# Output weights kept dequantised in DRAM, last loads on GpSimd's queue, first block projected in the last head

## The chip, the core and the metric

The kernel runs on one core of a Trainium2 chip. The metric is the device time of one execution in microseconds. The core has five engines with a queue of instructions each: TensorE (PE, with its weight loads as PEld), VectorE (DVE), ScalarE (ACT), GpSimd (POOL) and SyncE (SP). SP, ACT and POOL can issue DMA transfers; each has its own queue, and all transfers run on the same 16 DMA engines.

## What is computed

The input x has 2048 rows of 256. The block is a sandwich of attention and a mixture of experts:

```python
h  = layernorm(x)
q, k, v = h @ Wq + bq, h @ Wk + bk, h @ Wv + bv      # 16 heads of 128
o  = concat_h softmax(q_h k_h^T / sqrt(128)) v_h      # 2048 x 2048 scores per head
x  = x + layernorm(o @ Wo + bo)
g  = top-2 router of 8 experts on layernorm(x)
x  = x + layernorm(sum_e g_e * (silu(n @ Wg_e) * (n @ Wu_e)) @ Wd_e),  n = layernorm(x)
```

Wq, Wk, Wv and Wo come as codes (float32 values of a 4-bit grid) and a scale for each block of 32 rows; a weight is code times scale. Wo has 2048 rows (16 heads of 128) and 256 columns.

## The kernel before

**The loop.** The attention goes head by head, and in each head over 16 steps of 128 query rows (`for g in range(NS + 2)`, L740; h is the head, t the step). A step computes two halves of scores (`scores_half`, L478) on PE; DVE takes the maximum (L488), ACT the exponential (L499). In the next step ACT makes the float16 high part `ph` (L513) and DVE the low part `pl` in two halves (L528), the second one in the step after. SP transposes each with a DMA into `pth` (L516) and `ptl` (L534). `pl` has two buffers.

**PV.** Four steps make a block of 512 query rows. The product with V for a block is cut into eight units of six matmuls (`pv_part`, L546), two of them per step, and lags the scores by 13 units (`PVLAG`, L700). After the eighth unit POOL splits the result into two float16 parts `o` (L570, L571) and its queue stores them to `ot_d` in DRAM (L574). When the loop ends, the whole last block of head 15 (units `UEND + 1` to `UEND + 8`) is still to do.

**Side work.** `fill` (L582) puts the projections of q, k and v for this or the next head between the scores; `proj_qk` (L213) with `wide` leaves its cast and low part to POOL (L235, L236). `weight_steps` (L140) loads and dequantises Wq, Wk and Wv for the next pair of heads on POOL. Wo is loaded in eight pieces of two heads: pieces 0 to 2 in head 14 from POOL's queue (`load_wo_part`, L611), pieces 3 to 7 in head 15 (`late`, L709; `load_wo`, L628) with the scales from ACT's queue and the codes from SP's. POOL multiplies each piece into `wo` (L645). `late` also loads Wg and splits it (`split_gu`, L679), makes the bias row (`bias_row`, L647) and loads five of block 0's attention outputs back (`load_oi`, L689), all of it from SP's queue, on which the transposes are too.

**After the loop.** For each of four blocks of 512 rows: the output projection in two halves of 64 matmuls (`op_mm`, L811, on pieces `oi` of four heads), the norms (`ln_a` to `ln_c`), a transposition (`tr`), the router, and then gate/up and down matmuls (`gate_up`, L962; `down`, L999) in 11 chunks. Block 0 is projected whole before its gate/up; later blocks are projected among the gate/up matmuls of earlier ones. Wu and Wd are loaded and split in the same stretch (L1072 to L1135).

**What sets the order.** The order on each engine is the order in which the program is written; nothing reorders it. Tiles come from pools: a new tile of a tag takes a free buffer, or waits for the one that is released first. `kqv` has eight buffers of 4 KB per partition for the tag "kT" (K tiles and, late, other things) and eight for "v". A DMA from POOL's queue or SP's also waits, in its queue's order, for whatever frees its target.

Of the kernel before, what the change touches and what calls it, by code (L numbers as in the profile page):

```python
# [21 lines left out]
D = 256  # L22
# [15 lines left out]
def sandwich(  # L38
# [27 lines left out]
    ot_d = [dram.tile([128, 2, NH, 2, 256], HP, name=f"ot_d{b}") for b in range(4)]  # L66

# [145 lines left out]
    def proj_qk(which, h, b, tag="pj", wide=None):  # L213
        w = W[(h // 2, which)]
        bias = bqs[:, IX[which], h : h + 1]
        ps = proj_psum(tag)
        col = bass.ts(h % 2, 128)
        n = 0
        for kc in range(2):
            for hl in range(2):  # L220
                nc.tensor.matmul(
                    ps, w[:, kc, col], xnT[:, 4 * b : 4 * b + 4, hl * 2 + kc, :],
                    start=(n == 0), stop=(n == 3),
                )
                n += 1
        t = kqv.tile([128, 2, 512], HP, name=which + "T", bufs=8 if which == "k" else 2)
        if wide is None:
            nc.scalar.activation(t[:, 0, :], ps, AF.Identity, bias=bias)
            pending.append(lambda: nc.vector.scalar_tensor_tensor(
                t[:, 1, :], ps, bias, t[:, 0, :], ALU.add, ALU.subtract  # L230
            ))
        else:
            t32 = wide.tile([128, 512], F32, name="t32")
            nc.scalar.activation(t32, ps, AF.Identity, bias=bias)  # L234
            nc.gpsimd.tensor_copy(t[:, 0, :], t32)  # L235
            nc.gpsimd.tensor_tensor(t[:, 1, :], t32, t[:, 0, :], ALU.subtract)  # L236
        (Q if which == "q" else K)[(h, b)] = t
# [344 lines left out]
    def fill(h, t):  # L582
# [3 lines left out]
        if t in QK:  # L586
# [24 lines left out]
    def load_wo_part(j, part):  # L611
        hs = slice(2 * j, 2 * j + 2)
        if part == 0:
            wo_raw[j] = (
                stage.tile([128, 2, D], F32, name="wos", tag="st_s"),
                stage.tile([128, 2, D], F32, name="woc", tag="st_c"),
            )
        sc, cd = wo_raw[j]
        if part < 2:
            for b in (2 * part, 2 * part + 1):  # L620
                nc.gpsimd.dma_start(
                    out=sc[32 * b : 32 * b + 32],
                    in_=so[b : b + 1, hs].to_broadcast([32, 2, D]),
                )
        else:
            nc.gpsimd.dma_start(out=cd, in_=co[:, hs])

    def load_wo(j, pool, tags, bufs):  # L628
        hs = slice(2 * j, 2 * j + 2)
        sc = pool.tile([128, 2, D], F32, name="wos", tag=tags[0], bufs=bufs)  # L630
        for b in range(4):
            nc.scalar.dma_start(
                out=sc[32 * b : 32 * b + 32],
                in_=so[b : b + 1, hs].to_broadcast([32, 2, D]),
            )
        cd = pool.tile([128, 2, D], F32, name="woc", tag=tags[1], bufs=bufs)
        nc.sync.dma_start(out=cd, in_=co[:, hs])
        wo_raw[j] = (sc, cd)

    def dequant_wo(j):  # L640
        sc, cd = wo_raw.pop(j)
        if j % 4 == 0:
            wo.append(kqv.tile([128, 8, D], BF, name="wo", tag="v", bufs=8))
        hs = slice(2 * (j % 4), 2 * (j % 4) + 2)
        nc.gpsimd.tensor_tensor(wo[j // 4][:, hs], cd, sc, ALU.mult)  # L645
# [12 lines left out]
    def bias_row2(b3):  # L658
        pb2 = psA.tile([128, 512], F32, name="pb2", tag="pj")
        nc.tensor.matmul(pb2[:, :D], one3, b3, start=True, stop=True)  # L660
        nc.vector.tensor_tensor(crow, pb2[:, :D], crow, ALU.add)
# [27 lines left out]
    def load_oi(b, half, j, tag="kT"):  # L689
# [3 lines left out]
        nc.sync.dma_start(  # L693
# [9 lines left out]
    gw, crow = None, None  # L703
    gst = {}

    WO_LOAD = (0, 2, 4, 6, 8)
    WG_LOAD = (7, 9, 10, 11)

    def late(t):  # L709
        nonlocal gw, crow  # L710
        if t in WO_LOAD:
            load_wo(3 + WO_LOAD.index(t), kqv, ("kT", "kT"), 8)
        if t - 1 in WO_LOAD:
            dequant_wo(3 + WO_LOAD.index(t - 1))
        if t == 13:
            bias_row2(gst.pop("b3"))
        if t == 12:
            gst["b3"] = bias_row()
        if t == 9:
            proj_ctx.close()  # L720
            rp = ctx.enter_context(tc.tile_pool(name="gw", bufs=1, side="right"))
            gw = rp.tile([128, 2, 2, NCH, 128], F32R)
            crow = rp.tile([128, D], F32)
            nc.sync.dma_start(out=crow, in_=bo.partition_broadcast(128))
        if 10 <= t < 14:
            split_gu(gw, t - 10, gst.pop(t - 10), True)
        if t in WG_LOAD:
            i = WG_LOAD.index(t)
            gst[i] = load_gu(wg, i, kqv, "kT", 8)
        if t == 9:  # L730
            load_oi(0, 1, 0, "v")
        if 11 <= t < 15:
            load_oi(0, 0, t - 11)

    X1 = {}
    XV = x.rearrange("b (c p t) d -> p (b c) t d", p=128, t=4)

    defer = False
    prev2 = None
    for g in range(NS + 2):  # L740
        h, t = divmod(g, NT)
        live = g < NS
        if live:
            m = small.tile([128, 8], F32, name="m", bufs=6)
            s0 = scores_half(h, t, 0, m)
            if g == 0:
                proj_v(0, 0, 2)
                proj_v(0, 2, 2, "pv")
        if g == NS:
            load_oi(0, 1, 1)  # L750
            load_oi(0, 1, 2)
            load_oi(0, 1, 3)
        if prev is not None:
            recip(prev[2])
        if prev2 is not None:
            low_half(1, *prev2)
        flush()
        if defer:
            pv_unit(2 * g - 1)
            defer = False  # L760
        pv_unit(2 * g)
        if prev is not None:
            prev = (*prev, high_part(*prev))
        if live:
            s1 = scores_half(h, t, 1, m)
            negmax(m)
            p = softmax((s0, s1), m)
        if prev is not None:
            low_half(0, *prev)
        prev2 = prev  # L770
        first = live and (2 * g + 1 - PVLAG) % 8 == 0
        if not first:
            pv_unit(2 * g + 1)
        if live:
            fill(h, t)
        if first and h == NH - 1:
            defer = True
        elif first:
            pv_unit(2 * g + 1)
        if live:  # L780
            prev = (h, t, m, p)
        else:
            prev = None
        if live:
            weight_steps(h, t)
        if h == 0 and t in (8, 9):
            tail_consts(t - 8)
        if h == NH - 2 and t in (8, 12):
            dequant_wo(t // 4 - 2)
        if h == NH - 1 and t == 0:  # L790
            dequant_wo(2)
        if h == NH - 2 and t >= 4 and t % 4 < 3:
            load_wo_part(t // 4 - 1, t % 4)
        if h == NH - 1:
            late(t)
        if g == NS:
            X1[0] = kqv.tile([128, 4, D], F32, name="x1_0", tag="kT", bufs=8)
            nc.sync.dma_start(out=X1[0], in_=XV[:, 0])
    UEND = 2 * (NS + 2)

# [10 lines left out]
    def op_mm(b, half, js, tag="pj"):  # L811
        if js[0] == 0:
            if half == 0:
                AT[b] = uwp.tile([128, 4, D], F32, name="at", bufs=2)
# [54 lines left out]
    def ln_c(b):  # L869
        norm(AT[b], X1[b], MV2[b], R2[b])  # L870

# [197 lines left out]
    pv_unit(UEND)  # L1069
    soft_ctx.close()  # L1070
    nc.scalar.activation(sgv, ssc[:, 0:1], AF.Sigmoid)
    uwp = ctx.enter_context(tc.tile_pool(name="uw", bufs=1, side="right", reuse_waits="tile"))  # L1072
    ust = [load_gu(wu, i, uwp, "raw", 2) for i in range(2)]
    uw = uwp.tile([128, 2, 2, NCH, 128], F32R)
    for j in range(4):
        load_oi(1, 0, j)
    op_pass(0, 0, "s")
    op_pass(0, 1, "s")
    ln_a(0)
    ln_b1(0)  # L1080
    ln_b2(0)
    pv_unit(UEND + 1)
    pv_unit(UEND + 2)
    pv_unit(UEND + 3)
    pv_unit(UEND + 4)
    op_mm(1, 0, (0, 1), "s")
    pv_unit(UEND + 5)
    pv_unit(UEND + 6)
    pv_unit(UEND + 7)
    ln_c(0)  # L1090
    for i in range(2):
        split_gu(uw, i, ust[i], True)
        ust.append(load_gu(wu, i + 2, uwp, "raw", 2))
    for j in range(4):
        load_oi(1, 1, j)
    tr(0, 0, "s")
    tr(0, 1, "s")
    pv_unit(UEND + 8)
    router_a(0, "s")
    op_mm(1, 0, (2,), "s")  # L1100
    router_b(0, "s")
    for i in range(2, 4):
        split_gu(uw, i, ust[i], True)
    pt_ctx.close()
    tl = ctx.enter_context(tc.tile_pool(name="tl", bufs=1, reuse_waits="tile"))
    dw = tl.tile([128, 2, NCH, D], F32R)
    dsrc = wd.rearrange("e i d -> (e i) d").rearrange("(p c) d -> p c d", c=NCH)

    def load_d(c0):
        stg = uwp.tile([128, 4, D], F32, name="draw", tag="raw", bufs=2)  # L1110
# [13 lines left out]

    load_x1(1)
    d0 = load_d(0)
    router_c(0)
    op_mm(1, 0, (3,), "s")
    router_d(0, "s")
    d1 = load_d(4)  # L1130
    split_d(*d0)
    split_d(*d1)
    op_mm(1, 1, (0, 1, 2, 3), "s")
# [95 lines left out]
```

## Time and profile before

| | us |
|---|---|
| median of 3 runs (lowest to highest) | 1848.46 (1843.68 to 1856.08) |
| the profiled execution | 1847.86 |
| its span, first to last instruction | 1846.1 |
| busy in the span: PE, DVE, ACT, POOL | 1780.4, 1626.4, 1369.7, 948.7 |
| first and last `negmax` (L492) | 35.4 and 1557.7 |
| first gate/up matmul (L969) | 1613.4 |

In the lines of the profile, `L528` is line 528 of the kernel, `x3` a count, `out<-in` the tiles, and times are microseconds from the span's start, or durations. "SPq" is SP's queue: the row's duration is that of the issue, not of the transfer. In brackets stands how long the engine was idle before the row and what ended that. A wait for several things is put down to the one that came last. A PE row's end is modelled, so that matmuls in a row overlap by a part of their stated length. DMA share is the mean busy share of the 16 DMA engines; it can pass 1, since packets overlap.

### The profile page before, as it was taken

How to read it: one execution, taken by the hardware profiler on the slowest of the kernel's cores; microseconds unless marked ns; L12 is line 12 of the kernel's file. 1: busy time of each engine (PE TensorE's matmuls, PEld its weight loads, DVE VectorE, ACT ScalarE, POOL GpSimd, SP SyncE). 2: the span in 40 equal slices, each digit the busy share in tenths (PEclk: the TensorE clock that was granted, in tenths of full speed). 3: DMA queues.
4: the chain of work that ended last, by engine and by line, in shares of the span. 5: the costliest groups of instructions: out<-in, count | busy, mean ns of one | idle time of the engine just before them, and what ended most of it. 6: DMA issues, size and time to landing. Idle time of an engine off the chain costs nothing. (4 is left out here: it accounts for less than half of the span.)

```text
span 1846.1 us, 25409 instructions
## 1 busy us (share of the span) xinstructions
PE 1780.4 (96%) x8890; PEld 934.0 (51%) x8890; DVE 1626.4 (88%) x2267; ACT 1369.7 (74%) x1730; POOL 948.7 (51%) x929
## 2 busy tenths in 40 slices
PE   6899999999999999999999999999999888899998
PEld 4344444444444444444444444444444334588887
DVE  7999999999999999999999999999999886468566
ACT  5788888888888888888888888888888776223232
POOL 3366566556655565556555556565446432333232
PEclk9999999999999999999999999999999999999999
DMA  2999999999999999999999999999999999851000
GB/s 84 175 203 201 196 202 202 196 198 201 202 192 198 196 198 193 209 193 202 194 197 200 196 197 206 191 201 200 191 192 199 207 215 230 246 192 35 1 12 23
DMA packets 1091504, 330.70 MB, mean 179 GB/s; under 512 B 1070048, under 2 KB 1078064, under 8 KB 1091376
## 3 DMA queue, kind: packets, MB, share of 16 engines
q1 hardware_dynamic: 1078688, 298.14, 88.1%
q0 software_dynamic: 10544, 29.40, 5.9%
q10 hardware_dynamic: 2144, 1.54, 0.3%
q8 instruction: 70, 1.15, 0.2%
q14 instruction: 58, 0.48, 0.1%
HBM read 41.68 MB, written 18.87 MB: 33 GB/s over the span
## 5 line engine op out<-in xcount | busy, mean ns | idle before, releaser
L528 DVE SCALAR_TENSOR_TENSOR pl<-p,m,ph 128x1024 f16<-128x1024 f32 x512 | 722.9, 1412 | 40.5 <-DMA ptl<-pl 39.7
L499 ACT ACTIVATE p<-s,m,ssc 128x1024 f32<-128x1024 f32 x512 | 612.2, 1200 | 182.7 <-DVE m L492 165.8
L488 DVE TENSOR_REDUCE m<-s 128x1 f32<-128x1024 f32 x512 | 621.9, 1215 | 16.9 <-PE s L487 16.1
L513 ACT ACTIVATE ph<-p,m 128x2048 f16<-128x2048 f32 x256 | 513.0, 2004 | 69.6 <-issue 22.3
L554 PE MATMUL pv<-pth,v 128*128 128x512 f16 x2048 | 506.0, 380 | 9.6 <-POOL v L267 4.7
L554 PEld LDWEIGHTS <-v 128*128 128x128 f16 x3072 | 301.1, 98 | 376.9 <-POOL v L267 7.7
L483 PE MATMUL s<-kT,qT 128*128 128x512 f16 x1024 | 388.9, 380 | 22.5 <-ACT p L499 21.2
L484 PE MATMUL s<-kT,qT 128*128 128x512 f16 x1024 | 388.9, 380 | 0.0
L487 PE MATMUL s<-kT,qT 128*128 128x512 f16 x1024 | 305.0, 379 | 0.0
L554 PE MATMUL pv<-ptl,v 128*128 128x512 f16 x1024 | 253.2, 380 | 0.0
L235 POOL CAST qT<-t 128x512 f16<-128x512 f32 x63 | 78.7, 1250 | 240.6 <-ACT t L234 240.6
L266 POOL CAST v<-t 128x256 f16<-128x256 f32 (+1 forms) x105 | 46.3, 441 | 263.8 <-ACT t L265 263.8
L484 PEld LDWEIGHTS <-qT 128*128 128x128 f16 x1024 | 100.2, 98 | 138.4 <-issue 34.6
L267 POOL TENSOR_TENSOR v<-t,v 128x256 f16<-128x256 f32 (+1 forms) x105 | 160.6, 1530 | 8.5
L487 PEld LDWEIGHTS <-qT 128*128 128x128 f16 x1024 | 100.3, 98 | 121.5 <-issue 1.1
L483 PEld LDWEIGHTS <-qT 128*128 128x128 f16 x1024 | 100.2, 98 | 110.0 <-issue 1.1
L984 POOL TENSOR_TENSOR hh<-sg,hh 128x512 fp32r<-128x512 f32 x42 | 55.1, 1313 | 141.1 <-ACT hh L983 106.1
L983 ACT CAST hh<-sg 128x512 fp32r<-128x512 f32 (+1 forms) x45 | 27.5, 611 | 107.1 <-DVE sg L995 107.0
L499 ACT ACTIVATION_READ_ACCUMULATOR p<-s,m,ssc 128x1 f32 x512 | 99.0, 193 | 0.0
L571 POOL TENSOR_TENSOR o<-t,o 128x512 f16<-128x512 f32 x63 | 96.2, 1527 | 5.2
L235 POOL CAST kT<-t 128x512 f16<-128x512 f32 x60 | 65.0, 1083 | 57.9 <-ACT t L234 57.9
L236 POOL TENSOR_TENSOR kT<-t,kT 128x512 f16<-128x512 f32 x60 | 86.3, 1438 | 5.1
(186 smaller groups left out, 1831.8 us busy)
## 6 DMA issues: line engine op xcount, KB each, us to landing
oi<-ot_d SPq DMA_DIRECT2D x32, 512.0 KB, 5.0
ot_d<-o POOLq DMA_DIRECT2D x63, 256.0 KB, 4.3
pth<-ph SPq DMA_TRANSPOSE x256, 5.0
ptl<-pl SPq DMA_TRANSPOSE x256, 5.1
xt<-in_L_attn_x SPq DMA_DIRECT2D x4, 512.0 KB, 4.0
x<-in_L_attn_x SPq DMA_DIRECT2D x4, 512.0 KB, 4.7
st_s<-in_L_attn_wv_scales POOLq DMA_DIRECT2D x28, 64.0 KB, 4.3
st_c<-in_L_attn_wv_codes POOLq DMA_DIRECT2D x14, 128.0 KB, 4.3
```

The costliest lines, as they stand in the source:

```text
L235: nc.gpsimd.tensor_copy(t[:, 0, :], t32)
L236: nc.gpsimd.tensor_tensor(t[:, 1, :], t32, t[:, 0, :], ALU.subtract)
L267: nc.gpsimd.tensor_tensor(v[:, 1, sl, :], t32, v[:, 0, sl, :], ALU.subtract)
L483: nc.tensor.matmul(s[:, j, :], q[:, 0, qc], k[:, 0, :], start=True, stop=False)
L484: nc.tensor.matmul(s[:, j, :], q[:, 0, qc], k[:, 1, :], start=False, stop=False)
L487: nc.tensor.matmul(s[:, j, :], q[:, 1, qc], k[:, 0, :], start=False, stop=True)
L488: nc.vector.tensor_reduce(m[:, half : half + 1], s, AX.XY, ALU.max)
L499: nc.scalar.activation(p[:, bass.ts(i, 1024)], s, AF.Exp, bias=m[:, 2:3], scale=ssc[:, 0:1], accum_out=m[:, 3 + i : 4 + i],)
L513: nc.scalar.activation(ph, p, AF.Copy, scale=m[:, 6:7])
L528: nc.vector.scalar_tensor_tensor(pl[:, cs], p[:, cs], m[:, 6:7], ph[:, cs], ALU.mult, ALU.subtract)
L554: nc.tensor.matmul(ps, V[(h // 2, c // 4)][:, i % 2, c % 4, dc], d[:, :, c, :], start=(n == 0), stop=(n == 47),)
L571: nc.gpsimd.tensor_tensor(o[:, :, 1, :], halves(t32), o[:, :, 0, :], ALU.subtract)
```

## The change

Wo is dequantised during the loop: in the odd heads 1 to 11 one piece each in the last five steps, in head 13 two pieces, all on POOL and its queue (`wo_steps`), through the staging tiles of the other weights. The product goes to a DRAM tensor `wo_d` in bfloat16. In head 14 four loads bring it into `wo` (`load_wo`), and the bias row is made at that head's step 14.

In head 15 the q projections of blocks 1 to 3 come at steps 0, 1 and 2 instead of 0, 4 and 8, two of them into tiles of the tag "kT". All loads of heads 14 (`early`) and 15 (`late`) go to POOL's queue; SP's keeps the transposes. Block 0's projection moves into head 15: half 0 at steps 4, 5, 6 and 14, a quarter each, half 1 at step 15. Its first norm and residual come in the two steps after the loop. bo is added by POOL to the bias row. Behind the loop the remaining units of PV, block 1's projection, router and weight splits are put in a new order; half of the Wu pieces are split on DVE instead of POOL, and the first Wd loads come earlier, into buffers of their own.

```diff
-    def load_wo(j, pool, tags, bufs):
...
     def dequant_wo(j):
         sc, cd = wo_raw.pop(j)
-        nc.gpsimd.tensor_tensor(wo[j // 4][:, hs], cd, sc, ALU.mult)
+        w = stage.tile([128, 2, D], BF, name="wob")
+        nc.gpsimd.tensor_tensor(w, cd, sc, ALU.mult)
+        nc.gpsimd.dma_start(out=wo_d[:, 2 * j : 2 * j + 2], in_=w)
+    def wo_steps(h, t):
+        if h % 2 == 0 or h >= NH - 1:
+            return
+        if h < NH - 3:
+            plan = {11: (0, 1), 12: (2, 3), 13: (4,)}
+            j, done = h // 2, 15
+        elif t < 8:
+            plan = {i: (i,) for i in range(5)}
+            j, done = 6, 7
+        else:
+            plan = {8 + i: (i,) for i in range(5)}
+            j, done = 7, 15
...
+    def load_wo(q):
+        if q % 2 == 0:
             wo.append(kqv.tile([128, 8, D], BF, name="wo", tag="v", bufs=8))
+        hs = slice(4 * (q % 2), 4 * (q % 2) + 4)
+        nc.gpsimd.dma_start(out=wo[q // 2][:, hs], in_=wo_d[:, 4 * q : 4 * q + 4])
...
-        if t in QK:
+        if h == NH - 1:
+            if t < 3:
+                proj_qk("q", h, t + 1, wide=soft, slot="kT" if t > 0 else None)
+        elif t in QK:
...
+    GW_LOAD = {1: (0, "kT"), 5: (1, "v"), 6: (2, "v"), 7: (3, "kT")}
+    GW_SPLIT = {4: 0, 7: 1, 9: 2, 11: 3}
+    OI_LOAD = {
+        0: (0, 2, "kT"), 7: (1, 0, "kT"), 9: (1, 1, "v"), 11: (1, 2, "v"),
+        12: (0, 3, "kT"), 13: (1, 3, "kT"),
+    }
+    OI_USE = {4: (0, (0,)), 5: (0, (1,)), 6: (0, (2,)), 14: (0, (3,)), 15: (1, (0, 1, 2, 3))}
+    def early(t):
+        if 7 <= t < 11:
+            load_wo(t - 7)
+        if t in (12, 14):
+            load_oi(0, 0, t // 2 - 6, "v", nc.gpsimd)
+        if t == 14:
+            gst["b3"] = bias_row()
     def late(t):
...
+        if t == 3:
+            nc.gpsimd.dma_start(out=brow, in_=bo.partition_broadcast(128))
+            bias_row2(gst.pop("b3"))
+        if t in OI_USE:
+            op_mm(0, *OI_USE[t])
+        if t == 6:
+            nc.gpsimd.tensor_tensor(crow, crow, brow, ALU.add)
...
         if g == NS:
             X1[0] = kqv.tile([128, 4, D], F32, name="x1_0", tag="kT", bufs=8)
+            load_oi(1, 0, 0, "v", nc.gpsimd)
+            load_oi(1, 0, 1, "v", nc.gpsimd)
+            nc.gpsimd.dma_start(out=X1[0], in_=XV[:, 0])
+            ln_a(0)
+            ust = [load_gu(wu, i, kqv, "kT", 8, nc.gpsimd) for i in range(2)]
+        if g == NS + 1:
+            load_oi(1, 0, 2)
+            load_oi(1, 0, 3)
+            ust += [load_gu(wu, i, kqv, "kT", 8) for i in range(2, 4)]
+            ln_b1(0)
...
-    op_pass(0, 0, "s")
-    op_pass(0, 1, "s")
-    ln_a(0)
-    ln_b1(0)
+    d0 = load_d(0)
+    d1 = load_d(4)
+    op_mm(1, 0, (0, 1), "s")
     ln_b2(0)
+    split_gu(uw, 0, ust[0], True)
+    ln_c(0)
+    for e in range(1, 5):
+        pv_unit(UEND + e)
+    tr(0, 0, "s")
+    tr(0, 1, "s")
+    split_gu(uw, 1, ust[1], False)
+    op_mm(1, 0, (2, 3), "s")
+    for j in range(4):
+        load_oi(1, 1, j)
+    router_a(0, "s")
+    for e in range(5, 7):
+        pv_unit(UEND + e)
+    split_gu(uw, 2, ust[2], True)
+    router_b(0, "s")
+    split_gu(uw, 3, ust[3], False)
+    for e in range(7, 9):
+        pv_unit(UEND + e)
+    router_c(0)
+    split_d(*d0)
+    load_x1(1)
+    op_mm(1, 1, (0, 1), "s")
+    router_d(0, "s")
+    split_d(*d1)
+    op_mm(1, 1, (2, 3), "s")
```

## The prediction

> **What bounds the kernel now.** I read the busy times by stage first, then what each engine waited for in the last head, then the chain that ended last. The stretches are: head 14, head 15, from there to the first gate/up matmul, and the rest (columns: us; busy us and count of PE, weight loads, DVE, ACT, POOL; clock; DMA share; GB/s).
>
> ```profile
> 1358.00:1453.00 95.00, 92.23 (x434) 42.17 (x433) 88.23 (x113) 78.98 (x96) 51.51 (x52) 1.00 1.10 199
> 1453.00:1558.00 105.00, 89.60 (x400) 39.23 (x399) 82.39 (x108) 76.26 (x88) 38.20 (x28) 0.97 1.12 221
> 1558.00:1613.00 55.00, 47.53 (x343) 33.24 (x341) 22.36 (x62) 15.91 (x19) 13.50 (x11) 0.97 0.94 247
> 1613.00:1846.00 233.00, 223.92 (x1383) 194.54 (x1380) 154.44 (x340) 64.48 (x112) 72.06 (x56) 0.99 0.15 52
> ```
>
> Head 14, like heads 1 to 13 (93 to 97 us each), is full: PE is busy for 92 of 95 us. Head 15 has less projection work and yet takes 105 us; PE idles 15.4 us there and 7.5 us in the next 55. Those 22.9 us are all there is to win; the last 233 us hold nothing that the change touches. The clock is full everywhere. What DVE and PE waited for within head 15 (total us, times, longest):
>
> ```profile
> DVE pl L528 <- DMA ptl<-pl: 20.6, 11, 7.1
> PE s L483 <- ACT p L499: 15.4, 13, 5.2
> POOL wo L645 <- DMA woc<-in_L_attn_wo_codes: 30.1, 5, 9.0
> ```
>
> DVE busy 82.4 plus these 20.6 us is 103.0 of 105: head 15 runs at the pace of DVE and its wait. `pl` has two buffers, so step t's low half waits until the transposing DMA of step t-2 has landed; PE's 15.4 us are the echo, through m and the exponential. In the 1310 us of the loop before head 14's end the same wait sums to 13.0 us in 14 cases. On SP's queue one sees what is ahead of that DMA:
>
> ```profile
> 1519.28 0.88 SPq L724 DMA_DIRECT2D crow<-in_L_attn_bo  x1
> 1520.21 0.44 SPq L673 DMA_DIRECT2D gu_raw<-in_L_ffn_Wg  x1
> 1520.69 0.50 SPq L693 DMA_DIRECT2D oi<-ot_d  x1
> 1521.31 5.81 SPq L534 DMA_TRANSPOSE ptl<-pl  x1
> ```
>
> and in the chain that ended last this DMA is the longest piece, one landing per step from there to the drain (start, us):
>
> ```profile
> 1521.31 10.12 DMA ptl<-pl
> 1531.81 5.20 DMA ptl<-pl
> 1538.65 6.25 DMA ptl<-pl
> 1545.84 6.68 DMA ptl<-pl
> 1553.42 7.15 DMA ptl<-pl
> ```
>
> After the loop PE has gaps before the last `pth` and the last `oi`:
>
> ```profile
> 1561.74 8.90 PE L823 MATMUL op_s<-wo,oi 128*128 128x256 bf16 x80
> 1580.68 7.04 PE L554 MATMUL pv<-pth,v 128*128 128x512 f16 x24 [3.67 <-DMA pth<-ph]
> 1589.82 3.67 PE L823 MATMUL op_s<-wo,oi 128*128 128x256 bf16 x32 [2.10 <-DMA oi<-ot_d]
> ```
>
> **The change, part by part.** A PE matmul of 512 columns costs 0.2155 us in a row (12 in 2.75 us, the last one's tail of 0.38 taken off), an output-projection matmul 0.109 (64 in 6.99 us).
>
> *Wo through the loop.* Each of eight pairs of heads now costs POOL four issues of 0.546 us, one of 0.750, a multiply (1.75 median) and a store (0.70, the row of ot_d<-o, twice the size): 5.4 us. In heads 1 to 11 this falls to the last five steps, in head 13 to the whole head. POOL is busy 48 to 58 us per head of 94, so it hides there; without that cover the whole 43 us would count. The multiply waits for codes issued two steps (11 us) before; such codes from POOL's queue landed in 5.4 to 6.7 us, so it finds them. Behind it on POOL stand the next head's casts. What it adds to the DMA engines in heads 1 to 13 is eight times 256+256+128 KB, 5.2 MB. Price: stores and weights that POOL's queue already moves come to about 1.7 MB a head, 22 MB in 13 heads, for 13.0 us of that DVE wait, 0.6 us per MB: **+3 us**. Bounds: 0 (PE's slack takes it) and 24 us (rival C).
>
> *Head 14.* It loses three Wo pieces (1.5 MB) and takes four bf16 loads (1 MB) and two `oi` (1 MB), 0.5 MB more, and the bias row: 16 matmuls at 0.109, 1.7 us on a full PE. **+1 us**, between 0 and +2. The loads wait for V tiles that the last PV unit of head 13 frees one step before.
>
> *Head 15, removed.* Five Wo pieces of 512 KB: 20 ACT issues (0.33 each, 6.7 us of an engine with slack), five on SP, five POOL multiplies that were late for 30.1 us with nobody behind them. SP keeps only the transposes.
> *Head 15, bytes.* Before: 2.6 MB of Wo, 1.4 of Wg, 2.6 of `oi`, 0.1 of bo: 6.8 MB. After: 1.4 + six `oi` (3.1): 4.6 MB with bo. If a MB costs the DVE wait the same on any queue, 20.6/6.8 = 3.0 us per MB, the wait is 13.9 us; at POOL's loop price of 0.6 it is 2.8. I take 9, a bit above the middle, because the loop's eight stalls that I looked at mostly follow 256 KB or more on POOL's queue, and these loads are 512 KB.
> *The rule against it.* The Trainium skill (DMA: Bandwidth & Descriptors, "Issuing engines are not separate DMA queues") says that DMAs from any engine share the same 16 DMA engines and interleave, and that spreading them saves only the issuing time. By the rule the queue is worth SP's issues alone (15 of 0.4 to 0.9 us, some 8 us of SP, which is not what DVE waits for), and only the 2.2 MB less would count: wait 13.9. By the row above (10.12 us behind three loads, against a usual 5.1) being out of the queue counts also. The 9 stands between; by the rule my time would be 5 us later.
> *Head 15, added.* Block 0's half 0: 64 matmuls, 7.0 us on PE, at t=4, 5, 6 and 14. PE to the last scores: 372 matmuls (15 steps of 24, 12 of projection) at 0.2155 = 80.2, + 7.0 + 0.9 (bias to 128 rows) = 88 us: it fits under DVE. DVE gets the eviction and statistics, 0.75+0.75+0.22: 1.7, and a copy in place of an add (0.42). The q projections of blocks 1 to 3 move to t=0, 1, 2; three in a row cost PE 0.86 each, POOL 2.3 each: nothing, there is slack in both. Gate weights are split as before, at other steps.
> So DVE 82.4 + 1.7 + wait 9 + the 2.0 us of idle that remain today = 95.1. In the four steps with a quarter of half 0 PE needs 5.18 + 1.75 = 6.9 us where DVE's own work is 5.65; of these 5 us DVE's waits cover most, I add 1.4: **96.5 us (-8.5)**, between 88 (PE alone) and 102 (wait 13.9).
>
> *POOL's queue as the place of the loads.* The same codes landed in 5.9 us from POOL and 3.2 from SP. The Trainium skill (SBUF — State Buffer, "SBUF: two separate sides") warns that POOL-issued DMAs starve while DVE holds the shared port in a fast mode. By the row a load is 2.7 us later, by the rule some DVE instruction (1.2 to 1.4 us) more. Each `oi` has two steps or more before PE reads it, except (0,1,3): issued at t=13, read last at t=15. Nothing, by both. On POOL itself `oi` (0,0,3) at t=12 waits for the store of head 15's block 0 (issued at t=10, about 4.3 us); behind it only `oi` (0,1,3) is queued.
>
> *The drain.* Half 1 (64 matmuls, 7.0 us) follows the last scores. DVE's eviction at t=15 waits for it; behind it stand the reciprocal of step 15, the low halves of steps 14 and 15 and so the last two `ptl` and last `pth`. From the end of PE's last scores, T: PV 1.3, half 1 to T+8.3, eviction and statistics to T+10; reciprocal, ACT's ph (2.0) to T+12.5, its DMA landed by about T+18 to T+21. PE meanwhile has five PV units (6.5) and `op_mm(1,0,(0,1))` (3.5): covered to T+18.3. Then PV 5.2, transposes 0.9, projection 3.5, router 1.4, PV 2.6, router 0.4, PV 2.6, projection 3.5, 0.7, 3.5: 42.6 us of PE in all. Queues ahead of the last transposes: on SP none (before: three `oi`, 1.5 MB, and x); on POOL two `oi`, x and two Wu pieces (2.3 MB), which share the DMA engines with them. I add 3 us of waits (bounds 1 and 10): gate/up starts at T+45.6, which is 44 us after DVE's last negmax (T+1.5). Before: 1557.7 to 1613.4, 55.7 us. **-11.5 us**, of which 7.0 is half 0 gone into head 15.
>
> Sum: +3 +1 -8.5 -11.5 = -16. The profiled execution took 1847.86 us (span 1846.1), 0.6 below the median of 1848.46. **1832 us.**
>
> **Rivals.**
> A, *PE never idles*: the `ptl` wait vanishes as the loads leave SP's queue. For: in the loop it costs 1 us a head. Against: 512 KB loads beside transposes. The 22.9 us of idle go, loop cost 0: 1825; with the tails that the busy sums count (400 matmuls, 0.38 long at 0.2155 pitch) 1820.
> B, *the wait changes its name*: same DMA engines, so the `ptl` wait stays near 14 to 18 us, and in the drain PE waits 10 us for `pth` or `oi` behind the 2.3 MB. For: DMA share 1.12. -16 +7 +7: 1846, no change.
> C, *slower*: Wo's transfers hold up transposes all through the loop. A stall after POOL traffic cost DVE about 1.5 us (eight in heads 2 to 14, 0.4 to 2.6). Four groups of transfers a piece, eight pieces: 32; if half stall uncovered, 24 us in place of 3: 1853. It decides from 13 stalls on (19 us). Against: the loop holds 50 stores of 256 KB and as many loads from POOL already, and 14 waits in all.
> That it does nothing to the order is excluded: the projection of block 0 stands in head 15 in PE's program.
>
> **How the numbers follow.** Forecast 0.46 (1825 to 1840), A 0.12, B 0.20, C 0.22. The range 1819 to 1858 leaves out the end of A and the half of C in which more than 20 of the 32 groups stall (1832 - 3 + 30 = 1859). A measurement of this kernel can hardly tell less than 1%; faster by that is below 1830: A and a bit under half of the forecast, 0.33; slower by 1% (above 1867) is C with nearly all groups stalling, 0.11; the rest 0.56.
>
> **What would show it.** Wait of `pl` for `ptl` in head 15 near 9 us (right: 5 to 13); odd heads longer by about 0.5 us each; head 15 about 96 us; first gate/up 44 us after the last negmax, PE's gap before `pth` under 3 us; no PE wait for `oi` at t=4, 5, 6, 14, 15. Wrong if odd heads grow by 2 us or more, if POOL's waits delay `kT` or `v`, or if PE waits for block 1's `oi` in the drain.

## The result and the profile after

The changed kernel takes **1863.15 us** (median of 14 runs, 1856.28 to 1875.59) where the kernel before takes 1847.48 us (14 runs of the same series, 1843.68 to 1856.08): a ratio of **1.009, interval 1.0069 to 1.0111**. The forecast was 1832. The profiled execution took 1863.76 us (span 1861.5), 0.6 above its median, as the one before stood 0.6 below its own. In the series below, one execution of the kernel with its loads on ACT's queue and one of the kernel with the router's chain freed were over 1.5% slower than the fastest of their kernel; the medians and intervals leave both out, and since the second was the profiled one, its stages are left out too.

The windows of the changed kernel, for the same stages as before: heads 1 to 13, head 14, head 15, the drain up to the first gate/up matmul, the rest (columns as above):

```profile
133.00:1374.00 1241.00, 1220.54 (x5826) 568.77 (x5824) 1161.42 (x1457) 1038.17 (x1294) 742.49 (x763) 1.00 1.10 200
1374.00:1477.00 103.00, 96.83 (x447) 44.09 (x445) 88.06 (x113) 79.39 (x96) 42.95 (x42) 0.97 1.10 196
1477.00:1575.00 98.00, 92.44 (x461) 45.30 (x460) 85.88 (x111) 75.91 (x86) 36.19 (x34) 0.98 1.12 222
1575.00:1628.00 53.00, 41.63 (x266) 26.87 (x264) 28.23 (x60) 16.88 (x20) 18.15 (x15) 0.90 0.88 238
1628.00:1861.00 233.00, 224.13 (x1384) 194.70 (x1382) 154.30 (x340) 63.42 (x111) 67.32 (x54) 0.99 0.13 45
```

With the stages cut at `negmax` (L492 before, L496 after) and at the first gate/up matmul:

| stage | before, us | after, us | difference | forecast |
|---|---|---|---|---|
| to the start of head 14 | 1358.7 | 1374.1 | +15.5 | +3 |
| head 14 | 94.8 | 102.9 | +8.1 | +1 |
| head 15, to the last negmax | 104.3 | 98.0 | -6.3 | -8.5 |
| drain, to the first gate/up | 55.5 | 53.4 | -2.1 | -11.5 |
| the rest | 232.9 | 233.2 | +0.3 | 0 |

(The first gate/up matmul of the kernel before starts at 1613.2, so that its drain is 55.5 us and not the 55.7 that the forecast was reckoned from.) So head 15 did about what it was to do. Three other stages did not.

**The loop.** In heads 1 to 13 DVE waited for `ptl` this much (total us, times, longest), first in the kernel before, then in the changed one:

```profile
DVE pl L528 <- DMA ptl<-pl: 10.7, 13, 2.6
```

```profile
DVE pl L532 <- DMA ptl<-pl: 28.0, 34, 2.0
```

That is 17.3 us more, in 21 more stalls of some 0.8 us, and the stage is 15.5 us longer. The even heads grew, by 2.1 us each on average, the odd ones, where the new loads are, by 0.3. How little room there was can be read from the DMA queues in the same stretch of the kernel before (packets, MB, share of the 16 engines' time), where q1 carries the transposes and q0 what POOL issues:

```profile
q1 hardware_dynamic: 866363, 218.43, 102.0%
q0 software_dynamic: 8320, 23.41, 6.9%
```

The packets of the transposes alone take as much time as the 16 engines have. Packets overlap, so this does not show that nothing more fits, but every other byte runs beside a transpose. In the changed kernel q0 carries 28.52 MB in this stretch.

Most of the new stalls are not where the new loads are. The pieces of heads 1 to 11 have landed by step 14 of the odd head, and only the store of the product comes after. But in steps 0 to 4 of the even heads that follow (2 to 12) DVE stalls 14 times, for 12.4 us, 8 of them in steps 2 to 4; in the kernel before it did so twice in these five steps, for 0.9 us.

**Head 14.** Step 14 took 12.3 us instead of 5.6. PE there, in order of time:

```profile
1457.10 1.91 PE L222 MATMUL pj<-xnT,wk 128*128 128x512 f16 x4
1458.81 1.61 PE L558 MATMUL pv<-pth,v 128*128 128x512 f16 x6
1462.46 3.56 PE L666 MATMUL pb<-wo,bv 128*3 128x256 bf16 x16 [2.05 <-ACT t L238]
```

The bias row `pb` goes to the one PSUM buffer of the tag "pj" into which a k projection has just been written, so PE stands until ACT has copied that out (2.05 us); behind it stand the next scores, for which DVE waits 6.28 us. The 16 matmuls take 3.56 us, twice their 1.9 us in a place without idle time; the granted clock is 0.97 in this stage and 0.50 from 1462.5 to 1465.9.

**Head 15.** The wait for `ptl`, 20.6 us in 11 cases before, is:

```profile
DVE pl L532 <- DMA ptl<-pl: 6.4, 4, 3.6
```

PE waits for no `oi` there.

**The drain.** PE's gaps in it:

```profile
1595.66 7.00 PE L558 MATMUL pv<-pth,v 128*128 128x512 f16 x24 [6.19 <-DMA pth<-ph]
...
1622.80 1.03 PE L985 MATMUL pct_s<-ident,cx 128*128 128x128 f32 x4 [4.51 <-DVE cx L973]
1623.62 5.00 PE L746 MATMUL op_s<-wo,oi 128*128 128x256 bf16 x32
```

The two gaps are a late transpose and a late DVE, and after each the matmuls are slow: 24 in 7.00 us (5.2 at full speed) and 32 in 5.00 (3.66 elsewhere in the drain); the clock of this stage is 0.90, against 0.97 before. The transposes on SP's queue (start, us of the issue):

```profile
1582.80 4.35 SPq L538 DMA_TRANSPOSE ptl<-pl  x1
1587.24 1.82 SPq L520 DMA_TRANSPOSE pth<-ph  x1
1589.15 6.07 SPq L538 DMA_TRANSPOSE ptl<-pl  x1
```

ACT had finished `ph` at 1583.67; its transpose was started 3.6 us later, behind that of `ptl`, while `oi`, x and then Wu, 2.3 MB, came in from POOL's queue. In the router, DVE's own operations were long. DVE and POOL:

```profile
1613.19 1.90 DVE L951 TENSOR_TENSOR d<-mx 128x4 f32<-128x4 f32 x1
1615.01 0.15 DVE L952 TENSOR_TENSOR d<-mx 128x4 f32<-128x4 f32 x1
...
1619.23 3.52 DVE L973 TENSOR_TENSOR cx<-cw 128x512 f32<-128x512 f32 x1
```

```profile
1613.05 2.02 POOL L682 TENSOR_TENSOR uw<-gu_raw,uw 128x704 fp32r<-128x704 f32 x1 [14.00 <-ACT uw L680]
1619.10 0.71 POOL L578 DMA_DIRECT2D ot_d<-o_last  x1 [4.03 <-DVE cw L964]
1619.77 2.42 POOL L682 TENSOR_TENSOR dw<-draw,dw 128x1024 fp32r<-128x1024 f32 x1
```

`d`, 4 elements wide, ends when POOL's split ends; `cx` ends 0.6 us after one. In the kernel before both ran with no POOL instruction beside them:

```profile
1604.12 0.15 DVE L920 TENSOR_TENSOR d<-mx 128x4 f32<-128x4 f32 x1
...
1605.05 0.69 DVE L942 TENSOR_TENSOR cx<-cw 128x512 f32<-128x512 f32 x1
```

### The profile page after: what moved, and what is told of

It reads as the page before. It is cut to its first block, busy times and chain, and to the rows that moved or that the text cites. A ratio compares the mean times of both kernels' runs of the same rounds, so it can differ in the third digit from the quotient of the medians.

```text
span 1861.5 us, 25421 instructions
## 1 busy us (share of the span) xinstructions
PE 1785.7 (96%) x8890; PEld 935.9 (50%) x8890; DVE 1633.8 (88%) x2269; ACT 1370.0 (74%) x1730; POOL 965.1 (52%) x983
## 5 line engine op out<-in xcount | busy, mean ns | idle before, releaser
L492 DVE TENSOR_REDUCE m<-s 128x1 f32<-128x1024 f32 x512 | 621.7, 1214 | 25.0 <-PE s L491 24.4
L558 PE MATMUL pv<-pth,v 128*128 128x512 f16 x2048 | 506.9, 380 | 16.2 <-DMA pth<-ph 8.8
L487 PE MATMUL s<-kT,qT 128*128 128x512 f16 x992 | 376.4, 379 | 17.0 <-ACT p L503 16.3
L488 PE MATMUL s<-kT,qT 128*128 128x512 f16 x992 | 376.6, 380 | 0.0
L491 PE MATMUL s<-kT,qT 128*128 128x512 f16 x992 | 295.5, 380 | 0.0
L239 POOL CAST qT<-t 128x512 f16<-128x512 f32 x61 | 72.0, 1180 | 225.2 <-ACT t L238 225.1
L488 PEld LDWEIGHTS <-qT 128*128 128x128 f16 x992 | 97.0, 98 | 126.9 <-issue 26.2
L491 PEld LDWEIGHTS <-qT 128*128 128x128 f16 x992 | 97.2, 98 | 117.6 <-issue 1.0
L271 POOL TENSOR_TENSOR v<-t,v 128x256 f16<-128x256 f32 (+1 forms) x105 | 149.7, 1426 | 8.6
L487 PEld LDWEIGHTS <-qT 128*128 128x128 f16 x992 | 97.1, 98 | 105.9 <-issue 0.7
L250 PE MATMUL pj<-wv,xnT 128*128 128x256 bf16 x512 | 75.1, 275 | 9.4 <-DVE v L262 9.3
```

Source lines behind the costliest of these rows:

```text
L271: nc.gpsimd.tensor_tensor(v[:, 1, sl, :], t32, v[:, 0, sl, :], ALU.subtract)
L487: nc.tensor.matmul(s[:, j, :], q[:, 0, qc], k[:, 0, :], start=True, stop=False)
L488: nc.tensor.matmul(s[:, j, :], q[:, 0, qc], k[:, 1, :], start=False, stop=False)
L491: nc.tensor.matmul(s[:, j, :], q[:, 1, qc], k[:, 0, :], start=False, stop=True)
L492: nc.vector.tensor_reduce(m[:, half : half + 1], s, AX.XY, ALU.max)
L558: nc.tensor.matmul(ps, V[(h // 2, c // 4)][:, i % 2, c % 4, dc], d[:, :, c, :], start=(n == 0), stop=(n == 47),)
```

## The experiments

The theory after the traces was that three causes have nothing to do with each other: loads beside transposes in the loop, the bias row behind a projection in its bank, and in the drain loads and splits at the wrong time. The rivals: more instructions on a full POOL and PE (not the transfers) cost the loop its time; and the drain is bound by PE's own work. In the table each kernel stands with the kernel before of the same series; the stages are of its one profiled execution. The kernel before moved by 2.2 us from series to series, so a difference across series is also given with each kernel against the one before of its own series.

| kernel | median (runs) | before | ratio, interval | to head 14 | head 14 | head 15 | drain |
|---|---|---|---|---|---|---|---|
| changed | 1863.15 (14) | 1847.48 | 1.0090, 1.0069-1.0111 | 1374.1 | 102.9 | 98.0 | 53.4 |
| no Wo in heads 1-11 | 1851.55 (22) | 1849.65 | 1.0016, 0.9997-1.0034 | 1361.9 | 101.4 | 106.4 | 51.5 |
| its loads alone | 1870.14 (6) | 1849.65 | 1.0112, 1.0079-1.0144 | 1367.1 | 101.5 | 98.5 | 58.9 |
| loads on ACT's queue | 1853.53 (21) | 1849.65 | 1.0030, 1.0011-1.0048 | 1365.8 | 101.8 | 98.6 | 53.4 |
| bias row a step earlier | 1867.16 (6) | 1849.65 | 1.0108, 1.0070-1.0147 | 1371.6 | 95.8 | 103.5 | 63.1 |
| drain's loads moved | 1859.99 (6) | 1849.23 | 1.0074, 1.0052-1.0096 | 1377.4 | 99.8 | 100.8 | 49.4 |
| router's chain freed | 1858.79 (7) | 1849.23 | 1.0081, 1.0043-1.0118 | - | - | - | - |
| ACT's queue + bias row | 1849.49 (12) | 1849.23 | 1.0020, 0.9997-1.0043 | 1363.6 | 95.7 | 101.7 | 45.6 |
| all four edits | 1847.50 (12) | 1849.23 | 0.9998, 0.9976-1.0019 | 1364.9 | 95.7 | 105.2 | 46.6 |
| before, weights on ACT's queue | 1859.21 (6) | 1847.69 | 1.0055, 1.0034-1.0076 | 1368.3 | 92.6 | 103.5 | 58.0 |
| all four, weights on ACT's queue | 1848.42 (12) | 1847.69 | 1.0008, 0.9990-1.0026 | 1367.6 | 97.4 | 102.0 | 45.9 |
| all four, Wo one piece a step | 1873.44 (4) | 1847.69 | 1.0133, 1.0109-1.0156 | 1389.5 | 95.8 | 102.7 | 45.0 |

**The loop without Wo.** The pieces of heads 1 to 11 are neither loaded, multiplied nor stored; `load_wo` reads the two pieces made in head 13 instead, so the weights of heads 0 to 11 are left out of the output.

```diff
         if h < NH - 3:
+            return
...
-        nc.gpsimd.dma_start(out=wo[q // 2][:, hs], in_=wo_d[:, 4 * q : 4 * q + 4])
+        nc.gpsimd.dma_start(out=wo[q // 2][:, hs], in_=wo_d[:, 12:16])
```

> The changed kernel without the Wo pieces of heads 1 to 11 (no load, no multiply, no store; all four loads in head 14 read the two pieces made in head 13, so the output projection uses wrong weights of the same size). Theory: Wo's transfers through the loop hold up the transposes; heads 1 to 11 come back to the kernel before, the wait of pl for ptl in heads 1 to 12 from 22 to about 10 us, the time 10 to 13 us lower. Rival: the loop is longer for another reason (tiles placed elsewhere, POOL's loads in head 13 only); then less than 4 us.

The median is 11.6 us below the changed kernel (13.8 with each against its own series), the loop is 12.3 us shorter, and the wait in heads 1 to 13 is nearly back to its 10.7 us. In steps 0 to 4 of the even heads no stall is left.

```profile
DVE pl L532 <- DMA ptl<-pl: 13.6, 15, 2.3
```

**Its loads alone.** The same, but with the loads; multiply and store stay away, and `load_wo` reads head 13's pieces as above.

```diff
-        if t == done:
-            dequant_wo(j)
+        if t == done and j < 6:
+            wo_raw.pop(j)
+        elif t == done:
+            dequant_wo(j)
```

> As the run without Wo pieces in heads 1 to 11, but with their loads (512 KB each in the last five steps of the odd heads) and without multiply and store. If the loads' bytes or issues are what holds up the transposes, it is as slow as the changed kernel (within 3 us). If POOL's multiply and the store to DRAM are, it is as fast as the run without them (10 us or more below the changed kernel).

```profile
DVE pl L532 <- DMA ptl<-pl: 30.4, 38, 2.1
```

The median is 1870.14, and the interval overlaps that of the changed kernel. The loads alone bring back the whole wait (with 10 stalls, 10.3 us, in steps 0 to 4 of the even heads) and a median at least as high; POOL's multiply and the store are not needed for either. But the loop of this profiled execution is only 5.2 us longer than without the pieces, of the 12.3 in the changed kernel, so the length of the loop does not follow from the sum of this wait alone; what else adds to it is not shown. The drain, 58.9 us, holds a wait for `pth` of 11.1.

**The same loads from ACT's queue.** Bytes, steps and targets are kept; only the queue that starts them is another.

```diff
-            nc.gpsimd.dma_start(
+            nc.scalar.dma_start(
                 out=sc[32 * part : 32 * part + 32],
...
-            nc.gpsimd.dma_start(out=cd, in_=co[:, hs])
+            nc.scalar.dma_start(out=cd, in_=co[:, hs])
```

> The changed kernel with the Wo pieces loaded from ACT's queue instead of POOL's; multiply and store stay. If the bytes are the cost, the loop stays as long (within 3 us of the changed kernel). If it is POOL's queue (its issues of 0.55 us, or how its packets are served beside the transposes), the loop loses 5 us or more. ACT gains 40 issues of 0.33 us, which it has room for.

```profile
DVE pl L532 <- DMA ptl<-pl: 22.4, 31, 2.2
```

The median is 9.6 us lower (11.8 with each against its own series): most of the loop's price goes away though not a byte fewer is moved. This holds over several executions: with Wo's loads on ACT's queue head 14 starts at 1365.8, and at 1363.6 and 1364.9 in two later kernels with the same loop; with them on POOL's queue at 1374.1, 1371.6 and 1377.4. The wait falls by less, 5.6 us of the 17.3 here and some 11 in the other two; in steps 0 to 4 of the even heads 4 stalls of 2.1 us are left. Two things went away together with POOL's queue, how it serves packets and POOL's own time for issuing; no run separates them.

**The bias row in step 13**, where no projection stands before it.

```diff
-        if t == 14:
+        if t == 13:
             gst["b3"] = bias_row()
```

> The changed kernel with the bias row at step 13 of head 14 instead of 14. Theory: at step 14 it follows a k projection that holds the same PSUM bank until ACT, behind two exponentials, has read it; PE waits 2 us, cools, and the scores come 6 us late (step of 12.3 us). At step 13 nothing is projected: that step is at most 7.5 us, head 14 96 to 97 us instead of 102.9, the time 5 to 7 us lower. Rival: the loads of block 0 on POOL's queue in steps 12 and 14 are what makes head 14 long; then the time stays within 2 us.

The bias row runs at once, at full speed:

```profile
1447.20 1.91 PE L666 MATMUL pb<-wo,bv 128*3 128x256 bf16 x16
```

Head 14 takes 95.8 us instead of 102.9, and in all later kernels with this edit 95.7 to 97.4, against 99.8 to 102.9 without. Yet the median did not move (1867.16; the intervals overlap). The profiled execution lost the 7 us, and more, later: PE in the drain, and the drain's window with its clock of 0.81:

```profile
PE pv L558 <- DMA pth<-ph: 16.2, 1, 16.2
PE pct_s L985 <- DVE cx L973: 4.5, 1, 4.5
```

```profile
1571.00:1634.00 63.00, 41.66 (x253) 26.16 (x251) 27.28 (x60) 16.83 (x20) 17.70 (x15) 0.81 0.91 205
```

So head 14's gain was real, and in this execution the wait for the last transposes took it back. That pointed to the drain.

**The drain's loads moved.** X1 of block 0 is loaded in step 3 of head 15 into a tile of its own, which block 3's X1 takes later; the first two Wu pieces go to SP's queue behind the last transpose, and so POOL's split of the first one moves behind the transposition (`tr`).

```diff
+            x1e = lambda b: rp.tile([128, 4, D], F32, name=f"x1_{b}", tag="x1e")
+            gst["x1e"] = x1e
+            X1[0] = x1e(0)
+            nc.gpsimd.dma_start(out=X1[0], in_=XV[:, 0])
...
         if g == NS:
-            nc.gpsimd.dma_start(out=X1[0], in_=XV[:, 0])
             ln_a(0)
-            ust = [load_gu(wu, i, kqv, "kT", 8, nc.gpsimd) for i in range(2)]
         if g == NS + 1:
+            ust = [load_gu(wu, i, kqv, "kT", 8) for i in range(2)]
...
-    split_gu(uw, 0, ust[0], True)
     ln_c(0)
...
     tr(0, 1, "s")
+    split_gu(uw, 0, ust[0], True)
```

> The changed kernel with three transfers taken out of the drain's first 15 us: X1 of the first block is loaded in step 3 of head 15 (tile of its own, shared later with the last block), and the two first Wu pieces go to SP's queue behind the last transpose. If the loads on GpSimd's queue are what slows the last transposes: PE's wait before the last pth matmuls falls from 6.2 us (11.1 and 16.2 in two other executions) to 3 or less, the last transposes land within 6 us each, and the drain goes from 53.4 to 49-52 us; the median falls by 3 to 8 us. If the drain is bound by PE's own work or by the total of bytes, wait and drain stay within 1 us and the median within 2 us of the changed kernel's 1863.

PE's wait for `pth` is 2.4 us and the drain 49.4, as the first theory had it; but 3.0 us of a wait for `oi` came up behind it, and part of the gain is of another kind: the wait for `cx`, whose code this edit leaves as it was, is 1.7 us instead of 4.5.

```profile
1594.80 5.34 PE L558 MATMUL pv<-pth,v 128*128 128x512 f16 x24 [2.39 <-DMA pth<-ph]
...
1603.97 6.57 PE L746 MATMUL op_s<-wo,oi 128*128 128x256 bf16 x32 [2.95 <-DMA oi<-ot_d]
...
1623.49 0.66 PE L987 MATMUL pct_s<-ident,cx 128*128 128x128 f32 x4 [1.69 <-DVE cx L975]
```

The median, 3.2 us lower, is inside the intervals. Over the profiles, with X1 and Wu where the change put them the wait for `pth` was 6.2, 4.6, 11.1, 4.6, 16.2 and 1.0 us; in the four kernels with them moved 2.4, 2.4, 2.4 and 4.6, with about 3 us of waits for `oi` beside it in three of them. What these loads do in the drain is not a fixed price but a gamble: that they cause the long waits fits these numbers, and the 1.0 us shows that they need not.

**The router's chain freed.** The POOL split of Wu piece 2 goes before the PV units ahead of the router, the split of piece 3 behind `cx`, that of Wd piece 0 behind the router's transposes.

```diff
+    split_gu(uw, 2, ust[2], True)
     for e in range(5, 7):
         pv_unit(UEND + e)
-    split_gu(uw, 2, ust[2], True)
     router_b(0, "s")
-    split_gu(uw, 3, ust[3], False)
...
     router_c(0)
-    split_d(*d0)
+    split_gu(uw, 3, ust[3], False)
...
     router_d(0, "s")
+    split_d(*d0)
```

> The changed kernel with the weight splits moved off the router's chain: the GpSimd split of Wu piece 2 before the pv pieces ahead of the router, the split of piece 3 behind the router's cx, the split of Wd piece 0 behind the router's transposes. If VectorE's small operations are stretched by GpSimd's work beside them and by the split queued between them: d L951 falls from 1.90 to about 0.15-0.3 us, cx L973 from 3.52 to 0.7-1.0, PE's wait before pct from 4.51 to under 1.0, the 32 op matmuls behind it from 5.0 to 3.7 (no idle time, no slower clock), and the drain is shorter by 4 to 6 us. If those operations wait for the router's own data, PE's wait stays above 3 us. Medians: 1857 to 1860 by the first, 1863 by the second.

DVE and then PE in the kernel with all four edits, which has this one:

```profile
1603.58 1.91 DVE L953 TENSOR_TENSOR d<-mx 128x4 f32<-128x4 f32 x1
...
1607.43 0.69 DVE L975 TENSOR_TENSOR cx<-cw 128x512 f32<-128x512 f32 x1
```

```profile
1608.51 0.60 PE L987 MATMUL pct_s<-ident,cx 128*128 128x128 f32 x4
1608.94 3.66 PE L746 MATMUL op_s<-wo,oi 128*128 128x256 bf16 x32
```

`cx`, now with no split on POOL beside it, takes 0.69 us; PE does not wait, and its 32 matmuls take 3.66. The other kernels with this edit are alike. `d` did not follow: the POOL split that was moved waits for ACT's cast, which ACT does only after the router's first copy, so it ran from 1603.43 and lay beside `d` again.

That the edit freed `cx` is less clear than it looks. In the kernels with the drain's loads moved and with ACT's queue and the bias row, neither of which has the edit, the same POOL split starts 0.53 and 0.54 us into `cx`, as it does in the changed kernel (0.54), and `cx` took 0.69 us, where it took 3.52 in all five profiles of the changed kernel and the first four experiments. So a split beside `cx` does not always stretch it, and what decides is not shown. Of PE's 4.5 us, 2.8 come and go with that; the edit's sure part is the other 1.7, the wait that was left in those two kernels.

The median of this kernel (1851.6 to 1876.0 in seven runs) is too wide to show either: X1 and Wu are in their old place.

**Two edits, and all four.**

> The changed kernel with the Wo pieces of the loop on ACT's queue and the bias row in step 13 of head 14. The two alone gave 1853.9 and 1867.2. If the bias row's gain (head 14 went from 102.9 to 95.8 us) is real and was lost only because the last transposes fell beside loads (wait of 16.2 us), this gives 1846 to 1850 where the drain's wait is small and up to 1857 where it is large; head 14 takes 95 to 97 us. If moving the bias row only shifts the wait, 1853 to 1856.

Loads on ACT's queue and the bias row in step 13 give 1849.49 us, head 14 95.7, and this profiled execution had a wait for `pth` of only 1.0 us.

> All four edits together: Wo pieces on ACT's queue, bias row in step 13, X1 and Wu loads out of the drain, splits off the router's chain. If the three causes (loads holding up transposes in the loop, the bias row in the projections' bank, the drain's loads and splits) are separate and add up: 9 + 6 + 4 + 5 below the changed kernel's 1863, so 1836 to 1844, under both kernels. If the gain of one is given back in another: 1848 to 1856.

All four give 1847.50, 15.7 us below the changed kernel and level with the kernel before (0.9976 to 1.0019). The theory of causes that add up expected 1836 to 1844, the one in which a gain is given back elsewhere 1848 to 1856; the median lies between, next to the second. The gains do not add up in full. Its windows for head 14, head 15, drain and rest:

```profile
1365.00:1461.00 96.00, 94.40 (x451) 43.47 (x450) 88.01 (x113) 79.25 (x97) 42.59 (x42) 1.00 1.10 202
1461.00:1566.00 105.00, 93.90 (x462) 45.74 (x461) 86.34 (x112) 75.80 (x86) 35.18 (x35) 0.97 1.13 219
1566.00:1612.00 46.00, 39.69 (x259) 25.27 (x256) 25.02 (x60) 16.76 (x20) 12.60 (x11) 0.93 0.93 227
1612.00:1845.00 233.00, 224.10 (x1384) 194.71 (x1381) 155.18 (x340) 63.43 (x111) 70.79 (x56) 0.99 0.15 52
```

The drain is 9 us shorter than before the change. What is left of the loss stands in the loop, 6.2 us, and head 15 was no shorter than before in this execution (105.2 us). No version that was run beats the kernel before.

**Is it POOL's queue?** In the kernel before, all q, k and v weight pieces from ACT's queue, and the same in the kernel with all four edits.

```diff
-            nc.gpsimd.dma_start(
+            nc.scalar.dma_start(
                 out=sc[32 * piece : 32 * piece + 32],
...
-            nc.gpsimd.dma_start(out=cd[:, kc], in_=codes[bass.ts(kc, 128), cols])
+            nc.scalar.dma_start(out=cd[:, kc], in_=codes[bass.ts(kc, 128), cols])
```

> The kernel before with one thing changed: the loop's q, k and v weight pieces (some 110 loads) are started from ACT's queue instead of GpSimd's. The Wo pieces cost about 9 us less from ACT's queue than from GpSimd's. If that is a property of the queue beside transposes, these loads, several times as many, gain here too: VectorE's wait for ptl in heads 1 to 13 falls from 10.7 us to under 6, and the median by 3 to 8 us, to 1841 to 1846. If what counts is only the number of bytes beside transposes that already fill the DMA engines, the wait stays at 9 to 13 us and the median within 2 us of before; ACT's own issue time (some 110 issues) would then show as a loss of at most 3 us.

What DVE waited for most in heads 1 to 13, the row of the kernel before, and then all rows of the kernel with this edit:

```profile
DVE m L506 <- ACT p L499: 17.0, 62, 0.4
```

```profile
DVE m L506 <- ACT p L499: 26.7, 96, 0.6
DVE m L488 <- PE s L487: 9.4, 6, 1.6
```

The wait for `ptl` is gone, down to the last stall, though as many bytes run beside the transposes. And yet the kernel is 11.5 us slower, against both forecasts. DVE's wait for ACT's exponential is 9.7 us longer, nearly what the other lost. Nor do the transposes as a whole run freer. Their number and median time from issue to landing, in us, before and with this edit:

```profile
ptl<-pl SPq DMA_TRANSPOSE x209, 5.1
pth<-ph SPq DMA_TRANSPOSE x208, 5.0
```

```profile
ptl<-pl SPq DMA_TRANSPOSE x207, 4.8
pth<-ph SPq DMA_TRANSPOSE x206, 5.0
```

Only those that DVE waits for land a little sooner. So the run shows that the wait for `ptl` depends on the queue of the loads, and not that loads from ACT's queue leave transposes alone. Its heads 3 to 13 take 95.0 to 95.5 us, one like the other, where they took 93.2 to 96.3; steps 6, 8, 10 and 14 of the even heads are 0.6 to 0.7 us longer. That is work on ACT or an order that fits less well; the runs do not settle which.

A rival that no run tests is SP itself. It issues one transpose of each kind per step, and in heads 1 to 13 its issues alone take 91% of the time in the kernel before, 94% in the changed one and 86% with this edit. A late issue there makes a late landing, whatever the DMA engines do.

> The four edits together (1847.5) with the same move of the q, k and v weight pieces to ACT's queue, so that no load of heads 0 to 13 is on GpSimd's queue. By the queue theory heads 0 to 13 end at 1353 to 1360 (1364.9 with the four edits) and the median is 1838 to 1844; by the theory of bytes 1846 to 1850.

1848.42 us: no gain either, with 1.5 us of `ptl` wait in four stalls and the same even heads.

**Wo one piece a step.**

```diff
-            plan = {11: (0, 1), 12: (2, 3), 13: (4,)}
+            plan = {10 + i: (i,) for i in range(5)}
```

> The four edits together, with the Wo pieces of an odd head one to a step (steps 10 to 14) instead of two, two and one (steps 11 to 13). If a stall comes of two loads that meet in one step and hold up one transpose, spreading gains 1 to 4 us (1843.5 to 1846.5); if the sum of bytes counts, it stays within 1 us of 1847.5.

Neither theory: 1873.44 us, 26 us slower. ACT in an odd head:

```profile
782.66 0.32 ACTq L627 DMA_DIRECT2D wos<-in_L_attn_wo_scales  x1
783.10 2.00 ACT L517 ACTIVATE ph<-p,m 128x2048 f16<-128x2048 f32 x1 [5.26 <-POOL wv L185]
```

The piece of step 10 needs the staging tile that POOL frees in that step, with the dequantisation of wv. ACT stands in front of it, and `ph`, behind it on the same engine, starts 5.26 us late. This says nothing on spreading; it is what a load on a busy engine's queue costs when its tile is not free.

## Why the prediction was wrong

**Wo through the loop (+3): failed.** This is the largest miss. The stage is 15.5 us longer in the profile, and leaving out the pieces of heads 1 to 11 gave back 11.6 to 13.8 by the medians. The step priced a MB at 0.6 us, from the mean of all POOL traffic in the loop. The bytes were not the unit: there were 21 more stalls at 0.8 us for 5.1 MB, 3.4 us per MB, and with the same bytes from ACT's queue most of the price went away. The row that should have warned is the one of q1, 102% of the engines' time in packets of transposes alone. The argument that 50 stores and as many loads were already there with 14 waits was taken for spare room, which the mean of a loop does not show. Rival C came closest, with the point from which it decides, 13 stalls, but at 1.5 us each; it gave 1853, since it kept all the other gains. The sign that was named, odd heads longer by 2 us, was at the wrong place: the even heads grew. Why the stalls fall there, after the pieces have landed, stays open.

**The rule on issuing engines.** The Trainium skill (DMA: Bandwidth & Descriptors, "Issuing engines are not separate DMA queues") was weighed against a row for head 15. There it cannot be decided: the rule gave a wait for `ptl` of 13.9 us, the forecast 9, and the six executions with this head 15 have 3.7 to 16.2. In the loop the queue was worth some 9 us for the same Wo loads, three profiles against three. That is more than the rule gives if POOL's issuing time is hidden, as the prediction took it to be; whether it was hidden, no run tests. With all weight loads on ACT's queue no time was won. The page on the two sides of SBUF (SBUF — State Buffer, "SBUF: two separate sides"), which warns of loads from POOL's queue beside DVE, was taken to cost nothing; what it warns of is late loads, while what the runs show late are the transposes, and how they are held up is not shown.

**Head 14 (+1): failed.** The bias row was costed at 1.7 us of matmuls; +8.1 came, some 7 of it from its place. What the sum left out was the bank: the tile's tag has one buffer, and the same step writes a k projection to it first.

**Head 15 (-8.5): right in kind, with luck.** -6.3; the wait for `ptl` 6.4 us against a forecast of 9, inside 5 to 13, and 98.0 us against 96.5. Half 0 fits under DVE, and no `oi` was late. But this is the shortest of six executions with the same head 15: the others took 98.5 to 106.4 us, with waits of 3.7 to 16.2, over 13 in three. Their mean with it is 101.1, against 104.3 before.

**The drain (-11.5): failed.** PE reached its wait at 18.4 us after the last scores, where the forecast had 18.3; `pth` came at 24.6, beyond the 18 to 21 given. The forecast allowed 3 us for waits; there were 6.2 (`pth`), 4.5 (`cx`) and 0.7, and 3.1 us more by slow matmuls behind the two long waits. That is 11.5 us too many, and the gate/up matmuls stood at 57.3 us after the last scores instead of 45.6. (The stage is only 9.4 us off, since the last negmax, from which it is cut, also came 2.4 us later than forecast.) The slow matmuls could be read ahead: the prediction calls the clock full everywhere and costs these 24 at 5.2 us, though the line that it shows of the kernel before has them in 7.04, behind a wait of 3.67. The 2.3 MB on POOL's queue were seen and named in rival B, but priced low; the router's chain beside the splits was not looked at.

**Rivals A and B.** A needed PE never to be idle, and PE idled in the loop, in head 14 and in the drain. B's wait under another name came true in the drain (6.2 us for `pth`), not in head 15.

## What to carry to other kernels

Before adding a transfer to a loop, look at the DMA queues' share of the engines' time: where transposes alone add up to all of it, expect new loads to cost stalls, possibly later than the loads themselves, and do not price them by the mean per byte; try them from another queue. When a step gets a new instruction, look up the last writer of the buffer that it takes (a PSUM bank, a staging tile) and what is queued behind it, on PE and on ACT alike. A part that is gained ahead of a stage with uncertain waits can be lost in it: mend the wait as well, or the median will not show the gain.

## What was not expected of the hardware

- In the drain the DMA engines moved 95 GB/s for 9 us where transposes and POOL's loads of x and Wu ran together, with the engines busy throughout (the kernel with the bias row a step earlier, first row), against 379 in a stretch of loads alone (second row) and about 200 through the loop. Why is not shown.

```profile
1578.00:1587.00 9.00, 5.73 (x43) 3.93 (x41) 4.82 (x7) 2.08 (x3) 6.02 (x6) 1.00 1.18 95
1604.00:1610.00 6.00, 6.00 (x37) 3.74 (x36) 1.08 (x2) 1.70 (x3) 0.00 (x0) 0.90 1.06 379
```

- The whole wait of DVE for `ptl` in 13 heads, 10.7 us, went to nothing when the weight loads were started from ACT's queue, and the kernel was slower.
- A DVE instruction of 4 elements took 1.9 us instead of 0.15 beside a POOL instruction of 2.0, and ended with it; so it was in every kernel with the new drain (1.89 to 1.92 us). The Trainium skill describes such a lock of a port that DVE and POOL share (SBUF — State Buffer, "SBUF: two separate sides"). `cx`, 0.69 or 3.52 us with the same POOL instruction starting at the same place beside it, shows that this lock alone does not foretell what happens.
- After some idle times of PE its next matmuls ran slowly: 24 in 7.00 us instead of 5.2 behind 6.19 us, with a granted clock of 0.50 from 1592.2 to 1599.0. The Trainium skill has the clock halve after an idle window of about 3.4 us (TensorE: Matmul & The Clock Gate, "Part 1: The HAM clock gate"); in head 14 a wait of 2.80 us was already enough (the k projection 2 us behind it took 1.91 us instead of 1.03), while 24 matmuls behind a wait of 2.39 ran at full speed (5.34 us, with the drain's loads moved). So below 3.4 us the length of the wait alone did not decide. In the changed kernel's drain the clock made the two long waits some 30% dearer than their own length: 1.8 us on 6.2, 1.3 on 4.5.
